# Two shared experts with their inner units on the partitions: a four-layer gated model on one core

## The chip, the cores and the metric

The kernel runs on one core of a Trainium2 chip. The metric is the device time of one execution in microseconds (us), the median of several runs. Engines are named as in the profile: PE (TensorE: matrix products and transposes), PEld (its weight loads), DVE (VectorE), ACT (ScalarE), POOL (GpSimd) and SP (SyncE, which issues DMAs here). All products of the parts below are in fp32, which the profile counts as two PE instructions for each product.

## What is computed

2048 tokens of 512 channels pass four gated layers. Each adds `tanh(g) * attention(layernorm(x))` and then `tanh(g) * ffn(layernorm(x))`. Layer 0 has a quantised cross-attention and LoRA experts, layer 1 a linear attention and 64 experts, layer 2 an attention over channels and a dense network, layer 3 a recurrence and 8 experts. What matters here are the two feed-forward parts with experts. In layer 1 (E = 64 experts, 8 chosen per token, 176 inner units, 256 tokens per expert at most):

```python
def _shared_mlp(x, sh_gate, sh_up, sh_down):          # 512 -> 176 -> 512
    return jax.nn.silu(x @ sh_gate) * (x @ sh_up) @ sh_down
topk_idx, topk_w = _route(x, router_weight, e_bias)
moe_out = _moe_experts(x, topk_idx, topk_w.astype(x.dtype), w_gate, w_up, w_down)
out = moe_out + _shared_mlp(x, sh_gate, sh_up, sh_down)
```

and in layer 3 (8 experts, 2 chosen per token, 352 inner units; the shared expert has 2 x 352 = 704):

```python
y = jnp.einsum('ne,enh->nh', combine, eo)             # routed experts
sh = jax.nn.silu(x @ sw_gate) * (x @ sw_up)           # 512 -> 704
y = y + sh @ sw_down                                  # 704 -> 512
```

## The kernel before

The program is written in three stages, `front()` (layer 0), `middle()` (layer 1) and `back()` (layers 2 and 3). Tokens are worked on in four blocks of 512 (`BLK`), each of four tiles of 128 (`TB`); the residual stream x stays in SBUF. A scheduler places the instructions of each engine from the order in which the program issues them and from their dependencies. The author steers it by generators that are advanced by hand (`step`), by `behind(one, other)`, which fixes the order of two instructions without a wait, and by priorities.

Layer 1 in `middle()`. `attend1(blk, step)` runs the attention of a block and calls `step()` after each piece. `step()` advances `work()`, which for each half block (256 tokens, q = 0 to 6) that has left the attention runs `route1(q)`: layer norm, storing the normed tokens to `xnd` in DRAM, filling the same rows of two result arrays `acc[0]`, `acc[1]` with zeros (32 DMAs of 256 KB in all, on SP's queue), transposing the tokens into `tokens[blk]`, router logits, the choice of eight experts on DVE, and the indirect writes of the choices to `table` in DRAM, issued by POOL (L904). After q = 1 `work()` runs `shared1(0)`, and `attend1(1)` gets a `step` that advances twice for that. When the four blocks are through, `two` (`shared1` of blocks 1 and 2) is interleaved with `route1(7)`, the last half block, whose table writes end the routing. Then the whole table is loaded (`slots`), cast to `who` (L991), and the first tokens are gathered by POOL (`xg<-xnd,who`, L1007). The 64 experts follow, two tiles of 128 slots each (`Tile`, `down1`); their results are added by POOL's accumulating DMAs to `acc` (L1053). A remainder of 48 of the 176 inner units is multiplied there for two tiles side by side, at rows 0 and 64 of the array (L1044). After the experts comes `shared1(3)` with weights loaded again (`again`, on ACT's queue), and `combine()` in `back()` adds the two result arrays to x (L1104).

`shared1` itself, per block: the 176 units are taken as two halves of 88 (`I1H`), which lie on the partitions of the result. Per half four products for the gate and four for the up part (K = 128 each, 88 columns of weights stationary, 512 tokens moving), a silu on ACT, a product on DVE; then per tile of tokens two down products with K = 88 and an addition to x on DVE (L186).

Layer 3 in `back()`. While `ffn2` of layer 2's last block and the shared tiles run on PE, the attention tail of a block, `tail(blk)` (the recurrence `xattn3` on DVE, POOL and ACT, then `route`), is advanced by `step(n)`. `tail(3)` is left when the dense network is through; over it the first `SH0 = 6` shared tiles are issued, with `step(5)` at each `gate_up`, then `step(1000)` ends the tail. Then `cnt` and `pos` (the count of tokens per expert, on PE), the computation of each token's row, 32 table writes on POOL (L1533), the load of `slots`, the cast to `who` (L1552). `SH1 = 3` shared tiles are issued behind it. Then 39 routed tiles (`NS3`): each loads its expert's weights (`w<-in_w,wrow`, 2.2 MB, POOL, a ring of four) and gathers its 128 tokens (L1565), transposes them, runs `tile3`, and adds its result to the output by an accumulating indirect DMA (L1575). After each fifth routed tile one shared tile follows, seven in all.

`tile3` keeps tokens on the partitions: `gate_up` takes a tile of 128 tokens as the stationary operand and moves 352 weight columns, 8 products; a silu on ACT (L1425) and a product with the scale on DVE (L1427) give `h`; `transposed` makes three PE transposes (L1434) and two copies (L1436 on DVE, the other on ACT) of it; `down` makes three products of 512 columns, and `evac` copies the result, by turns on DVE and ACT (L96, L98), before the DMA that adds it to the output (L1465 for shared tiles). The down products of a tile are issued after the next tile's gate and up. A shared tile is two such parts with 352 units each: 16 products, six transposes, six down products.

Pools that count: PSUM has four banks of 512 columns for `mm`, two for transposes (`tr`) and two for `ac` (down products of layer 3); `t2` has eight SBUF buffers of 2 KB per partition, used by all stages for short-lived tiles; `wpool` and `b8` have six of 8 KB each.

Of the kernel before, what the change touches and what calls it, by code (L numbers as in the profile page):

```python
# [31 lines left out]
I1H = I1 // 2  # L32
# [4 lines left out]
SH0, SH1 = 6, 3  # L37
# [6 lines left out]
def flamingo_kernel(ctx: ExitStack, tc: tile.TileContext, a):  # L44
# [533 lines left out]
    def middle():  # L578
        with ExitStack() as st:
# [36 lines left out]
            zero = lp.tile([P, C], F32, tag="zero", name="zero")  # L616
            nc.gpsimd.memset(zero, 0.0)
            empty = lp.tile([P, P, 2], F32, tag="slots", name="empty")
# [8 lines left out]
            shg = rwsh[:, KC * E1 : KC * (E1 + I1)].rearrange("p (k o) -> p k o", k=KC)  # L627
            shu = rwsh[:, KC * (E1 + I1) : KC * (E1 + 2 * I1)].rearrange("p (k o) -> p k o", k=KC)
            for dst, key in ((rw, "rwT1"), (shg, "shg1"), (shu, "shu1")):
                nc.sync.dma_start(dst, a[key].rearrange("p (k o) -> p k o", k=KC))  # L630
            shd = lp.tile([I1H, 2, C], F32, tag="shd1", name="shd1")
# [166 lines left out]
            def route1(q):  # L798
# [4 lines left out]
                if q % 2 == 0:  # L803
                    pool, tag = (wpool, "w") if blk == 1 else (b8, "b8")
                    tokens[blk] = pool.tile([P, KC, BLK], F32, tag=tag, name=f"xnT_f1{blk}")
                xnT = tokens[blk][:, :, ts(q % 2, S)]
                for i in range(2):
                    t = ti + i
                    one = nc.sync.dma_start(xnd[ts(t, P), :], xns[i])
                    for u in range(2):  # L810
                        behind(nc.sync.dma_start(acc[u][ts(t, P), :], zero), one, "not all of them at once")
                    transpose4(xnT[:, :, ts(i, P)], xns[i], f"f1{q}_{i}")
# [104 lines left out]
            def shared1(blk, shg, shu, after=None):  # L917

                xnT = tokens[blk]
                hT = [t2.tile([P, BLK], F32, tag="t2", name=f"shT{blk}_{h}") for h in range(2)]  # L920
                for h in range(2):
                    pg = mmtile(f"shg{blk}_{h}")
                    pu = mmtile(f"shu{blk}_{h}")
                    for ps, wt in ((pg, shg), (pu, shu)):
                        one = matmul_k(
                            ps[:I1H, :], [wt[:, k, ts(h, I1H)] for k in range(KC)], [xnT[:, k, :] for k in range(KC)]
                        )
                        if after is not None:
                            behind(one, after, "beside the sum of the results")
                        yield  # L930
                    act = t2.tile([P, BLK], F32, tag="t2", name=f"sha{blk}_{h}")
                    nc.scalar.activation(act[:I1H, :], pg[:I1H, :], AF.Silu)
                    nc.vector.tensor_tensor(hT[h][:I1H, :], pu[:I1H, :], act[:I1H, :], ALU.mult)
                    yield
                for i in range(TB):
                    ps = mmtile(f"shd{blk}_{i}")
                    matmul_k(ps, [hT[h][:I1H, ts(i, P)] for h in range(2)], [shd[:, h, :] for h in range(2)])
                    t = blk * TB + i
                    last_add[:] = [add_scaled(t, ps, tg[:, 5:6])]
                    yield  # L940

            def work():

                for q in range(2 * NB - 1):
# [3 lines left out]
                    if q == 1:  # L948
                        yield from shared1(0, shg, shu)
# [7 lines left out]
            for blk in range(NB):  # L957
                attend1(blk, (lambda: (step(), step())) if blk == 1 else step)
# [4 lines left out]
            two = (x for blk in range(1, NB - 1) for x in shared1(blk, shg, shu))  # L963
# [12 lines left out]
            again = l2.tile([P, 2, KC, I1], F32, tag="shgu1", name="shgu1")  # L976
            for g, key in enumerate(("shg1", "shu1")):
                nc.scalar.dma_start(again[:, g], a[key].rearrange("p (k o) -> p k o", k=KC))


            slots = lp.tile([P, P, 2], F32, tag="slots", name="slots")
# [8 lines left out]
            who = lp.tile([P, P], I32, tag="who", name="who")  # L990
            one = nc.vector.tensor_copy(who, slots[:, :, 0])  # L991
            behind(one, last_add[0], "the table comes late")

            I1R = I1 - P
            rows_of = (slice(0, I1R), slice(HD * 2, HD * 2 + I1R))

# [95 lines left out]
            for _ in shared1(NB - 1, again[:, 0], again[:, 1], latest[0]):  # L1092
# [168 lines left out]
    def back():  # L1261
        with ExitStack() as st:
# [140 lines left out]
            for h in range(2):  # L1403
                for kk in range(2):
                    w = late.tile([P, 4 * I3], F32, tag=f"shgu{h}_{kk}", name=f"shgu{h}_{kk}")
                    nc.sync.dma_start(w, a["shgu3"][h][:, kk * 4 * I3 : (kk + 1) * 4 * I3])
                    shgu += [w[:, k * 2 * I3 : (k + 1) * 2 * I3].rearrange("p (g i) -> p g i", g=2) for k in range(2)]
# [7 lines left out]
            def gate_up(xTt, wgu, scale, name):  # L1415
# [11 lines left out]
                one = nc.vector.scalar_tensor_tensor(h, act, scale, pu[:, 0:I3], ALU.mult, ALU.mult)  # L1427
                return h, one

            def transposed(h, name):  # L1430
# [4 lines left out]
                hT = late.tile([P, 3, P], F32, tag="hT3", name=f"hT3_{name}", bufs=4)  # L1435
# [4 lines left out]
            def down(name, hTs, wds, add):  # L1440
                ps = ac.tile([P, C], F32, tag="ac", name=f"d3_{name}")
                pairs = [(hT[:cn, n, :], wd[n][:cn]) for hT, wd in zip(hTs, wds) for n, (_, cn) in enumerate(chunks)]
                matmul_k(ps, [l for l, _ in pairs], [r for _, r in pairs])
# [7 lines left out]
            def tile3(name, parts, wds, add):  # L1451
                hs = []
# [238 lines left out]
```

## Time and profile before

The median of three runs is 2926.47 us (2926.19 to 2926.68). The profile is of another execution, of 2930.48 us.

| | us |
|---|---|
| median of the runs | 2926.47 |
| profiled execution, its own time | 2930.48 |
| its span on the page | 2928.6 |
| mean granted clock of TensorE | 0.967 |
| PE busy | 2713.0 (93%) |
| layer 1's experts, 1043.9 to 1621.2 | 577.3 |
| layer 3's routed tiles, 2472 to 2922 | 450.0 |

The span begins at 0 with the first instruction that the profiler saw. A row of a timeline gives the start, the time that the group took, engine, line, operation, output and inputs, partitions and columns, the count, and in brackets the idle time of the engine before it and what ended that. In a table of windows each row is a stretch of the span, with its length and the busy time of each engine in it. The tenths of section 2 of the page cut the span into 40 slices of 73.2 us. The busy time of PE is modelled, so distances between starts are the better measure of what a product takes.

### The profile page before, as it was taken

What the parts mean: (1) busy time and instruction counts of PE and PEld (TensorE: products, weight loads), DVE (VectorE), ACT (ScalarE), POOL (GpSimd) and SP (SyncE); (2) the same over time, 40 slices, a digit from 0 to 9 for tenths busy, and PEclk for the clock granted to TensorE, in tenths of its full rate; (3) what the DMA queues carried; (4) which work ended last, traced back from release to release, by engine and by line L of the source; (5) the groups of instructions that cost most, each with busy time, mean ns of one, the idle gap of its engine ahead of it and who ended that gap; (6) DMA issues with size and microseconds to landing.
All of it is one profiled execution on the core that took longest, in us unless ns stands there. A gap on an engine that the chain in (4) does not pass through costs nothing. (4 is left out here: it accounts for less than half of the span.)

```text
span 2928.6 us, 30661 instructions
## 1 busy us (share of the span) xinstructions
PE 2713.0 (93%) x10918; PEld 1478.7 (50%) x10918; DVE 1315.5 (45%) x3574; ACT 711.0 (24%) x1616; POOL 942.4 (32%) x849
## 2 busy tenths in 40 slices
PE   7888978899899989999999899898999888999998
PEld 3444544464555445555555344344444554555554
DVE  7566665353556522222222631767566861111111
ACT  2534343011111123333333211222222220111111
POOL 1102010104324455555555110322223326333232
PEclk9999989899899999999999999999999999999999
DMA  5000000110101168999998722121221214777775
GB/s 198 22 4 19 28 25 19 45 54 6 58 23 37 54 189 204 216 227 224 215 221 204 226 87 75 40 101 36 83 90 36 94 44 159 241 258 235 225 249 142
DMA packets 104746, 345.09 MB, mean 118 GB/s; under 512 B 22426, under 2 KB 24858, under 8 KB 96787
## 3 DMA queue, kind: packets, MB, share of 16 engines
q0 software_dynamic: 50448, 168.71, 23.3%
q1 hardware_dynamic: 51123, 169.19, 16.8%
q10 hardware_dynamic: 3024, 5.24, 0.5%
q8 instruction: 87, 1.43, 0.2%
q14 instruction: 64, 0.52, 0.1%
HBM read 283.42 MB, written 69.80 MB: 121 GB/s over the span
## 5 line engine op out<-in xcount | busy, mean ns | idle before, releaser
L175 PE MATMUL gu<-w,eb 128*128 128x352 f32 x1024 | 326.5, 462 | 0.0
L1053 POOL DMA_INDIRECT acc<-eb,who x128 | 203.9, 1593 | 197.7 <-DVE eb L96 174.5
L175 PE MATMUL h2p<-xnT_f,p 128*128 128x512 f32 x512 | 227.4, 600 | 6.0 <-issue 3.9
L175 PEld LDWEIGHTS gu<-w,eb 128*128 128x128 f32 x1024 | 185.7, 191 | 83.6 <-issue 2.3
L175 PE MATMUL o2f<-p,h 128*128 128x512 f32 x512 | 226.1, 597 | 0.7 <-ACT h L1166 0.7
L471 ACT ACTIVATE pr<-pr,n 128x256 f32<-128x256 f32 x256 | 127.9, 501 | 157.2 <-DVE n L466 151.8
L175 PEld LDWEIGHTS h2p<-xnT_f,p 128*128 128x128 f32 x512 | 97.5, 192 | 125.1 <-issue 120.7
L175 PEld LDWEIGHTS o2f<-p,h 128*128 128x128 f32 x512 | 97.1, 191 | 120.3 <-issue 116.8
L904 POOL DMA_INDIRECT table<-pay,rowi x128 | 125.7, 982 | 93.2 <-DVE hit L895 47.8
L1007 POOL DMA_INDIRECT xg<-xnd,who x128 | 135.1, 1055 | 58.2 <-PE ehp L1033 27.3
L1427 DVE SCALAR_TENSOR_TENSOR h_r<-a_r,slots,u_r 128x352 f32<-128x352 f32 x39 | 22.6, 580 | 225.2 <-ACT a_r L1425 118.3
L159 PEld LDWEIGHTS tr_xg<-ident,xg 128*128 128x128 f32 x668 | 78.2, 142 | 87.3 <-issue 78.9
L186 DVE SCALAR_TENSOR_TENSOR x<-o2f,tg,x 128x512 f32<-128x512 f32 x64 | 47.8, 748 | 165.2 <-PE o2f L175 165.2
L175 PE MATMUL d_r<-w,hT_r 128*128 128x512 f32 (+1 forms) x234 | 115.3, 606 | 7.3 <-DVE hT_r L1436 6.0
L1044 PE MATMUL ed<-w,eb 128*128 128x512 f32 x256 | 120.8, 593 | 0.9 <-DVE eb L1034 0.9
L159 PE MATMUL tr_xg<-ident,xg 128*128 128x128 f32 x668 | 104.9, 280 | 17.4 <-DMA xg<-xnd,who 17.4
L1421 PE MATMUL g_r<-w,xgT 128*128 128x352 f32 x312 | 119.0, 463 | 0.0
L1421 PE MATMUL u_r<-w,xgT 128*128 128x352 f32 x312 | 118.0, 460 | 0.0
L96 DVE COPY eb<-ed 128x512 f32<-128x512 f32 x64 | 44.3, 692 | 158.5 <-PE ed L1044 158.5
L1166 ACT ACTIVATE h<-h2p,b 128x512 f32<-128x512 f32 x64 | 43.1, 687 | 290.1 <-PE h2p L175 289.9
L1023 DVE SCALAR_TENSOR_TENSOR eb<-eb,slots,gu 128x176 f32<-128x176 f32 x128 | 50.2, 392 | 139.1 <-ACT eb L1022 139.1
L478 PE MATMUL pt<-ident,pr 128*128 128x128 f32 x512 | 88.1, 293 | 19.9 <-ACT pr L471 16.2
(396 smaller groups left out, 4984.7 us busy)
## 6 DMA issues: line engine op xcount, KB each, us to landing
w<-in_w SPq DMA_DIRECT2D x64, 960.0 KB, 6.9
p<-in_p SPq DMA_DIRECT2D x64, 512.0 KB, 5.5
xnd<-xn_f SPq DMA_DIRECT2D x32, 256.0 KB, 2.7
acc<-zero SPq DMA_DIRECT2D x32, 256.0 KB, 3.0
more<-acc SPq DMA_DIRECT2D x32, 256.0 KB, 4.8
wd<-in_wd SPq DMA_DIRECT2D x64, 96.0 KB, 6.1
x<-in_x SPq DMA_DIRECT2D x16, 256.0 KB, 7.0
ctxTb<-in_ctxT SPq DMA_DIRECT2D x4, 1024.0 KB, 5.0
```

What stands on the lines that cost most here:

```text
L96: nc.vector.tensor_copy(dst, src)
L159: nc.tensor.transpose(ps[:, k, :], src[:, ts(k, P)], ident)
L175: one = nc.tensor.matmul(ps, lhsT[k], rhs[k], start=(k == 0), stop=(k == n - 1))
L186: return nc.vector.scalar_tensor_tensor(xt[i], ps, scale, xt[i], ALU.mult, ALU.add)
L471: nc.scalar.activation(pr[:, nt, :], pr[:, nt, :], AF.Exp, bias=n16[:, nt, h : h + 1], scale=-1.0, accum_out=s16[:, nt, h : h + 1],)
L478: nc.tensor.transpose(pt_ps[:, lt, nt, :], pr[:, nt, ts(lt, P)], ident)
L904: one = nc.gpsimd.indirect_dma_start(out=table[:, :], out_offset=bass.IndirectOffsetOnAxis(ap=row_i[:, i, j : j + 1], axis=0), in_=pay[:, ...
L1007: nc.gpsimd.indirect_dma_start(out=xg, out_offset=None, in_=xnd[:, :], in_offset=bass.IndirectOffsetOnAxis(ap=who[:, c : c + 1], axis=0), ...
L1023: nc.vector.scalar_tensor_tensor(self.h, self.h, slots[:, c, 1:2], gu[:, I1 : 2 * I1], ALU.mult, ALU.mult)
L1044: one = nc.tensor.matmul(ps[n], t.hT[rows, k, :], wd[k][rows], start=(k == 0), stop=(k == 1))
L1053: nc.gpsimd.indirect_dma_start(out=acc[n][:, :], out_offset=bass.IndirectOffsetOnAxis(ap=who[:, t.c : t.c + 1], axis=0), in_=t.x, in_offse ...
L1421: nc.tensor.matmul(ps[:, 0:I3], xTt[:, k, :], wgu[k][:, g, :], start=(k == 0), stop=(k == KC - 1))
```

## The change

Both shared experts are put in one form: inner units on the partitions, 128 at a time, 512 tokens moving, and the units that are left over from gate and up joined in one product.

- Layer 1, `shared1`: 128 units of gate, 128 of up, and one product of 112 columns that holds the last 48 of gate (rows 0 to 47 of the result), 16 columns of zeros, and the last 48 of up (rows 64 to 111). Down goes by pairs of tiles: one full product of K = 128 for each, and the two of K = 48 side by side at rows 0 and 64 (`behind` fixes their order). The host lays out the weights as `shgu1` (one load for gate and up) and `shd1` with the last 48 rows twice.
- Block 0's `shared1` is taken out of `work()` and put ahead of blocks 1 and 2 in `two`, behind the attention; `attend1(1)` has a single `step`. `tokens[0]` has a buffer of its own, `tokens[1]` one of `wpool`, the others of `b8`.
- Layer 3, `shared3`: a generator of eight pieces per block. The first is the joined remainder (64 of gate, 64 of up: four products of 512 columns, `step(2)`), five are 128 units of gate and up (eight products, `step(5)` each), two are the down products of a pair of tiles (ten full, two of K = 64 side by side, `step(3)`). No transposes. `SH0 = 14` pieces stand over `tail(3)`, `SH1 = 8` after the table, then one after each third routed tile, which is ten. `tile3` serves routed tiles alone.
- The zero tile of layer 1 is a short-lived one of `t2`, and the zero fills of `acc` copy from the 128 zero rows at the end of `xnd`, DRAM to DRAM. `slots` and `who` are in the pool `l2`, which opens after the attention.

```diff
-SH0, SH1 = 6, 3
+SH0, SH1 = 14, 8
...
-            zero = lp.tile([P, C], F32, tag="zero", name="zero")
+            zero = t2.tile([P, C], F32, tag="t2", name="zero")
...
-                    pool, tag = (wpool, "w") if blk == 1 else (b8, "b8")
+                    pool, tag = ((lp, "tokens"), (wpool, "w"), (b8, "b8"), (b8, "b8"))[blk]
...
-                        behind(nc.sync.dma_start(acc[u][ts(t, P), :], zero), one, "not all of them at once")
+                        fill = nc.sync.dma_start(acc[u][ts(t, P), :], xnd[NT : NT + P, :])
+                        behind(fill, one, "not all of them at once")
...
+                pg = products("shg", slice(0, P))
+                nc.scalar.activation(act[0], pg, AF.Silu)
+                yield
+                pu = products("shu", slice(P, 2 * P))
+                nc.vector.tensor_tensor(hT[0], pu, act[0], ALU.mult)
+                yield
+                ps = products("shr", slice(2 * P, I1W))
+                nc.scalar.activation(act[1][rest1, :], ps[0:I1R, :], AF.Silu)
+                for n in range(2):
+                    pick = lambda x: x.rearrange("p (t n q) -> p t n q", n=2, q=P)[:, :, n]
+                    nc.vector.tensor_tensor(
+                        pick(hT[1][rows_of[n], :]), pick(act[1][rest1, :]), pick(ps[rest1, :]), ALU.mult
+                    )
+                yield
+                for i in range(0, TB, 2):
+                    ps = [mmtile(f"shd{blk}_{i + n}") for n in range(2)]
+                    last = None
+                    for k in range(2):
+                        for n in range(2):
+                            rows = rows_of[n] if k else slice(0, P)
+                            one = nc.tensor.matmul(
+                                ps[n], hT[k][rows, ts(i + n, P)], shd[rows, k, :], start=(k == 0), stop=(k == 1)
+                            )
+                            if last is not None:
+                                behind(one, last, "remainders side by side")
+                            last = one
+                    latest[:] = [last]
+                    for n in range(2):
+                        last_add[:] = [add_scaled(blk * TB + i + n, ps[n], tg[:, 5:6])]
                     yield
...
                     yield from route1(q)
-                    if q == 1:
-                        yield from shared1(0, shg, shu)
...
-                attend1(blk, (lambda: (step(), step())) if blk == 1 else step)
+                attend1(blk, step)
...
-            two = (x for blk in range(1, NB - 1) for x in shared1(blk, shg, shu))
+            two = (x for blk in range(NB - 1) for x in shared1(blk, shgu))
...
-            for _ in shared1(NB - 1, again[:, 0], again[:, 1], latest[0]):
+            for _ in shared1(NB - 1, again, latest[0]):
...
+            def shared3():
+                half = [slice(FD * n, FD * n + FD) for n in range(2)]
+                scale = tg[:, 7:8]
+                for blk in range(NB):
+                    xb = [xT[blk][:, k, :] for k in range(KC)]
+                    hT = late.tile([P, 6, BLK], F32, tag="shT3", name=f"shT3_{blk}")
+                    for m in (5, *range(5)):
+                        nm = f"{blk}_{m}"
+                        act = t2.tile([P, BLK], F32, tag="t2", name=f"sa3_{nm}")
+                        pg = mmtile(f"sg3_{nm}")
+                        if m == 5:
+                            matmul_k(pg, [w[:, 10 * P :] for w in shgu], xb)
+                            nc.scalar.activation(act[half[1], :], pg[half[0], :], AF.Silu)
+                            for n in range(2):
...
+                            step(2, one)
+                        else:
+                            pu = mmtile(f"su3_{nm}")
+                            for ps, c in ((pg, m), (pu, m + 5)):
+                                matmul_k(ps, [w[:, ts(c, P)] for w in shgu], xb)
+                            nc.scalar.activation(act, pg, AF.Silu)
+                            one = nc.vector.scalar_tensor_tensor(hT[:, m, :], act, scale, pu, ALU.mult, ALU.mult)
+                            step(5, one)
+                        if later:
+                            down(*later.pop())
+                        yield
+                    for i in range(0, TB, 2):
+                        ps = [ac.tile([P, C], F32, tag="ac", name=f"sd3_{blk}_{i + n}") for n in range(2)]
+                        last = None
+                        for m in range(6):
+                            for n in range(2):
+                                rows = half[n] if m == 5 else slice(0, P)
+                                one = nc.tensor.matmul(
+                                    ps[n], hT[rows, m, ts(i + n, P)], shd[m][rows, :], start=(m == 0), stop=(m == 5)
+                                )
+                                if last is not None:
+                                    behind(one, last, "remainders side by side")
+                                last = one
+                        for n, copy in enumerate((nc.vector.tensor_copy, nc.scalar.copy)):
+                            t = blk * TB + i + n
+                            y = t2.tile([P, C], F32, tag="t2", name=f"ys3_{t}")
+                            one = copy(y, ps[n])
+                            if n == 0:
+                                step(3, one)
+                            nc.gpsimd.dma_start(out=a["out"][ts(t, P), :], in_=y, accum_op=ALU.add)
+                        yield
...
-            for t in range(SH0):
-                shared(t)
+            more = shared3()
+            for n in range(SH0):
+                next(more)
             step(1000)
...
             for n in range(SH1):
-                shared(done)
-                done += 1
+                next(more)
             for n in range(NS3):
                 routed(n)
-                if n % 5 == 4 and done < TT:
-                    shared(done)
-                    done += 1
-            while done < TT:
-                shared(done)
-                done += 1
+                if n % 3 == 2:
+                    next(more, 0)
+            for _ in more:
+                pass
             down(*later.pop())
```

## Prediction

> **What bounds the kernel now.** I read the page first, then a table of windows by stage, then the timelines of the places where TensorE stands still. The chain that ended last is cut off after its last DMA here, so the bound is read stage by stage.
>
> ```profile
> PE 2713.0 (93%) x10918; PEld 1478.7 (50%) x10918; DVE 1315.5 (45%) x3574; ACT 711.0 (24%) x1616; POOL 942.4 (32%) x849
> ...
> PE   7888978899899989999999899898999888999998
> ```
>
> TensorE is the bound, with dips in the tenths. The windows give span, then busy us of PE, PEld, DVE, ACT, POOL, then granted clock, DMA share, GB/s: attention blocks 1, 2, 3 of layer 1 (blocks of 512 tokens), the wait for its expert table, its experts, then layer 3's attention tail, its table, its routed tiles.
>
> ```profile
> 650.19:781.01 130.82, 120.01 (x581) 68.10 (x580) 65.71 (x291) 17.56 (x28) 46.36 (x49) 0.90 0.10 33
> 781.01:881.71 100.70, 91.73 (x534) 54.71 (x532) 53.32 (x222) 13.70 (x24) 32.51 (x34) 0.97 0.09 32
> 881.71:985.05 103.34, 92.92 (x533) 56.21 (x532) 60.37 (x254) 15.09 (x25) 39.56 (x44) 0.95 0.15 49
> 985.05:1043.91 58.86, 46.67 (x131) 20.04 (x129) 27.88 (x138) 5.80 (x8) 36.48 (x38) 0.92 0.26 84
> 1043.91:1621.20 577.29, 576.43 (x2298) 331.89 (x2297) 157.55 (x382) 187.90 (x447) 331.25 (x250) 1.00 0.89 211
> ...
> 2282.76:2411.09 128.33, 112.15 (x420) 69.00 (x419) 90.00 (x151) 34.35 (x49) 42.44 (x39) 0.93 0.20 56
> 2411.09:2472.00 60.91, 47.11 (x151) 27.14 (x151) 11.24 (x39) 6.81 (x15) 42.25 (x43) 0.91 0.37 112
> 2472.00:2922.00 450.00, 438.80 (x1487) 255.51 (x1486) 80.16 (x149) 62.21 (x149) 136.67 (x116) 1.00 0.72 231
> ```
>
> Block 1, which holds shared block 0, takes 29 us more than its neighbours. The experts and the routed tiles are TensorE-bound; the two table stages are not. PE's timeline (start, duration, group, idle before it) at the table wait of layer 1, and POOL's:
>
> ```profile
> 1023.11 7.29 PE L175 MATMUL shd<-shd,shT 88*128 88x512 f32 x16
> 1042.04 1.94 PE L159 MATMUL tr_xg<-ident,xg 128*128 128x128 f32 x8 [11.64 <-DMA xg<-xnd,who]
> ```
>
> ```profile
> 1029.82 0.97 POOL L904 DMA_INDIRECT table<-pay,rowi  x1 [0.30 <-issue]
> 1034.63 1.06 POOL L1007 DMA_INDIRECT xg<-xnd,who  x1 [3.83 <-DVE who L991]
> ```
>
> The shared products end 11.64 us before the first gathered tokens: POOL's 32 table writes, 1.27 us apart from 990.2 on, set the end of this stage. In layer 3 likewise (PE's timeline):
>
> ```profile
> 2448.36 5.32 PE L175 MATMUL d_s<-shd,hT_s 128*128 128x512 f32 x12
> 2461.72 1.54 PE L1434 MATMUL h3t_s<-ident,h_s 128*128 128x128 f32 x6 [8.04 <-DVE h_s L1427]
> ...
> 2470.89 1.09 PE L159 MATMUL tr_xg<-ident,xg 128*128 128x128 f32 x4 [5.76 <-DMA xg<-xnd,who]
> ```
>
> Of all filler, only what TensorE does outside these two waits is worth its time. Last, the price of two 48-row products side by side (PE's timeline):
>
> ```profile
> 1619.11 1.10 PE L1044 MATMUL ed<-w,eb 128*128 128x512 f32 x2 [0.47 <-DVE eb L1034]
> 1620.14 1.13 PE L1044 MATMUL ed<-wd,eb 48*128 48x512 f32 x4
> 1621.20 3.67 PE L175 MATMUL shg<-xnT_f,shgu 128*88 128x512 f32 x8
> 1624.70 1.88 PE L175 MATMUL shu<-xnT_f,shgu 128*88 128x512 f32 x4
> ```
>
> From start to start: a 512-column fp32 product (two instructions) takes 0.86-0.88 us whether 88 or 128 rows or columns are used; the pair of 48-row products takes 1.06 for both.
>
> **What the Trainium skill says.** "TensorE: Matmul & The Clock Gate", Part 3: products on different row groups run at once, the pack lasting about as long as one. The trace agrees in part: 1.06 us against 1.72 for two, but 0.86 for one; I use 1.06. Part 1 of that page: after an idle window of about 3.4 us the clock falls to half. The trace has clocks of 0.90 to 0.92 in just the windows with long idles. Its architectural detail: ACT's and DVE's queues are strict FIFO. It agrees: h_s stands 8.04 us behind the cast of `who`. "DMA: Bandwidth & Descriptors", rules for kernel authors: an accumulating DMA must wait for the earlier one's semaphore; POOL shows that wait at 2561.50 and 2570.64 (2.38 and 2.83 us, released by out_dram).
>
> **Part by part**, on the profiled execution's 2930.5 us (span 2928.6 and 1.9 around it), which lies 4.0 above the median.
>
> *1. Products of layer 1's shared expert.* Per block 24 products of 0.86 = 20.6 us (16 gate and up, 8 down) become 12 + 4 of 0.86 and 2 pairs of 1.06: 15.9. So 4.75 us per block, 19.0 over four.
>
> *2. Block 0's shared work leaves attention block 1.* Its 20.6 us of PE go, and the doubled step with them, which put DVE work of routing and sharing into the attention's own chain and let the clock fall. If block 1 becomes like 2 and 3 (mean 102.0) it saves 130.8 - 102.0 = 28.8. Bounds 20.6 (PE work only) and 31; I take 28.8.
>
> *3. Table wait of layer 1.* Filler goes from two blocks (41.2) to three short ones (3 x 15.85 = 47.5): 6.3 us more, inside the 11.64 idle. Cost 0; without that cover 6.3. Block 0's two products for h, silus and four adds (0.75 each) now stand on DVE and ACT among route 7's; behind them waits the last `hit` and behind that POOL's writes. The writes need 41 us, and the hits come a microsecond or two ahead of POOL by my order of DVE: 0, bounds -3 and +5.
>
> *4. Zero fills* go from SBUF to DRAM, 32 of 256 KB on SP (now 3.0 us to landing). DRAM to DRAM is not in the trace. They are read first after 1054 us, and the last is issued before 985, so 0 to 10 us each would be hidden; a ctxT load (1 MB, 5.0 us) stands behind some. SP waited 307 us for xn_f in this stage, so the queue has room. I take 0; bounds 0 and +5. The single load of `again` on ACT's queue for two, and four loads of layer 3's shared weights for four, cost the same.
>
> *5. Block 3's shared work after the experts.* 4.75 us less before the adds of the results, which stand behind its adds on DVE; TensorE resumes at 1650.44 after 8.15 us for xn_a. If the results' loads (4.8 us) come late instead, the gain is lost: 0 to 4.75; I take 4.
>
> *6. Products of layer 3's shared expert.* Before, per tile of 128 tokens: 16 of 352 columns at 0.592 = 9.47, six transposes of 0.11, six down of 0.86 = 5.15: 15.3; 244.5 for 16. After, per block: 44 of 0.86 and two times (10 full of 0.86 and one pair of 1.06) = 57.1; 228.2 for four. So -16.3: gate and up cost the same, transposes and remainders go. On DVE two copies (0.42) and two products (0.58) per tile become 5 wide products and 2 half ones per block: less.
>
> *7. Under the attention tail* 14 steps (94.8 us) stand for six tiles (91.7). The chain over DVE, POOL and ACT (about 20.8 us for each chunk of channels) sets this stage, and steps come at each product as before. The copy of a tile's result holds DVE until its products end, 4.3 us before; it now waits for a pair of 9.64 but seldomer. I take -2; bounds -8 and +8.
>
> *8. Table wait of layer 3.* From `cnt` to `who` is 50 us of POOL in both. Eight steps (57.0 us) replace three tiles (45.8). Some 11 us of idle move ahead of `who`, since the wide products' DVE steps stand behind its cast, and four PSUM banks fill; then about 10 us of ready products cover the gather, whose 5.76 us of idle go. Take -1; bounds -3 and +5.
>
> *9. Routed tiles.* Shared work here falls from 7 x 15.3 = 107.0 to 228.2 - 94.8 - 57.0 = 76.4: -30.6, all in a stage with PE at 438.8 of 450. Fewer waits of d_s for hT_s (2.4 us in this stage): -1. But the last nine tiles have no shared step between them. One then takes 8.69 us on PE, and its accumulate waits for the one before: issues at 2550.75, 2561.50, 2570.64, 2578.67 are 9.3 apart where weights are loading. Five such tiles x 0.6 = +3; bounds 0 and +10.
>
> Sum: -28.8 + 0 + 0 - 4 - 2 - 1 - 28.6 = -64.4. The profiled 2930.5 becomes 2866; at the median 2862.
>
> **The rivals.**
> *Only products count.* The 19.0 + 16.3 = 35.3 us of TensorE work go, and no idle is filled: block 1's surplus moves to block 2 or to the table wait, where route 7's hits come late. For it: DVE is a strict queue with new work there. Against: 11.64 us of idle await filler. 2926.5 - 35.3 = 2891.
> *New waits in layer 3.* The tail +8 and the end +10 in place of -2 and +3: 17 less, 2879. For it: DVE 90 of 128 us in the tail, and copies queued behind longer products. Against: fewer DVE instructions.
> *Slower: the accumulate chain.* Each of 39 tiles waits for its forerunner's landing, from about 9.3 us now. With layer 1 giving 32.8, the kernel is slower by over 0.2% once routed tiles take 450 + 32.8 + 5.9 = 489 us, 12.5 us each; at 13 us it ends near 2926.5 - 32.8 + 57 = 2951. For it: DMA share rises from 0.72 to 0.72 x 450/421 = 0.77. Against: 8 to 10.8 us is all I see, and at the end, with the weights loaded, the tiles follow at 8.7.
> *It doesn't do what it says.* If the order keeps block 0 in the attention and the shared tiles' idles, 2926. The build's order of instructions speaks against it: the shared transposes are gone and PE's instructions fall.
>
> **How the numbers follow.** Forecast 0.60, only products 0.15, new waits 0.16, slower 0.05, nothing 0.04. A measurement here tells about 0.2% (5.9 us) from no change. Faster 0.91, same 0.04, slower 0.05. The range runs from 2846 (block 1 at -31, combine -4.75, tail -6, table -3, routed -36, rounded) to 2892, just past the products alone.
>
> **What would show it.** Block 1's window at 100 to 104 us with no shg in it (step 2). Idle of 4 to 7 us ahead of the first tr_xg in layer 1, at the same distance from block 3's end (3). Shared blocks of 15.9 (1, 5). `cnt` within 8 us of its place after the combine (7); idle near 11 us before `who` and none for xg (8); routed window 418 to 424 (9). Wrong if route 7's last table write slips by over 5 us, if PE waits at each shared pair, or if out_dram releases every accumulate.

## The result and the profile after

The changed kernel takes 2891.94 us (median of four runs, 2890.79 to 2895.47) against 2926.33 for the kernel before: a ratio of 0.9885, 95% interval 0.9868 to 0.9902. It is faster by some 34 us, about half of the 64 that the sum had given, at the very edge of the range, which ended at 2892. The profiled execution has a span of 2893.7 us, 34.9 less than before.

The page after, the rows that answer to those shown of before:

```profile
PE 2676.9 (93%) x10630; PEld 1427.0 (49%) x10630; DVE 1312.1 (45%) x3542; ACT 698.7 (24%) x1574; POOL 940.9 (33%) x849
...
PE   7889978899898999999999899898999988999998
```

TensorE has 36.1 us less to do and the span is 34.9 shorter, as if only the products had counted. The stages tell otherwise. Windows after (span, then busy us of PE, PEld, DVE, ACT, POOL, granted clock, DMA share, GB/s): attention blocks 1 to 3, the table wait of layer 1, then the attention tail of layer 3, its table up to the cast of `who`, from there to the first routed gate, and the routed tiles:

```profile
650.53:753.91 103.38, 92.52 (x533) 56.16 (x532) 60.38 (x256) 13.70 (x24) 39.71 (x41) 0.95 0.13 42
753.91:857.36 103.45, 92.99 (x533) 57.08 (x532) 60.46 (x256) 13.80 (x24) 39.53 (x41) 0.95 0.10 32
857.36:962.10 104.74, 94.27 (x533) 57.59 (x532) 60.19 (x254) 15.08 (x25) 39.56 (x44) 0.93 0.15 49
962.10:1021.98 59.88, 53.59 (x148) 22.20 (x146) 32.46 (x149) 6.99 (x10) 34.80 (x36) 0.97 0.23 71
2253.14:2396.33 143.19, 128.54 (x372) 63.58 (x371) 94.80 (x152) 33.93 (x37) 42.23 (x39) 0.92 0.20 63
2396.33:2446.14 49.81, 39.85 (x98) 16.78 (x96) 7.99 (x30) 5.43 (x8) 36.17 (x38) 0.96 0.20 54
2446.14:2461.89 15.75, 13.74 (x28) 6.08 (x29) 3.59 (x6) 0.60 (x1) 7.33 (x8) 0.80 1.03 360
2461.89:2887.00 425.11, 403.74 (x1311) 223.28 (x1311) 69.96 (x127) 54.03 (x127) 135.81 (x116) 1.00 0.75 240
```

Cut at the same instructions in both traces (wo is the attention's output product, tr_xg the transposes of the first gathered tokens, gu and ed the experts' gate/up and down products, o2f the last products of layer 2's dense network, d_r a routed tile's down products):

| stage | before | after | difference | forecast |
|---|---|---|---|---|
| attention block 1 | 130.8 | 103.4 | -27.4 | -28.8 |
| attention blocks 2 and 3 | 204.0 | 208.2 | +4.2 | 0 |
| last wo product to first tr_xg | 57.4 | 59.9 | +2.5 | 0 |
| experts of layer 1 (gu to the last ed) | 576.8 | 575.2 | -1.5 | 0 |
| to the first product of layer 2 | 29.8 | 25.6 | -4.1 | -4 |
| layer 2 | 626.2 | 628.0 | +1.8 | 0 |
| last o2f product to cnt | 134.4 | 143.2 | +8.7 | -2 |
| cnt to the first routed gate | 62.4 | 65.6 | +3.2 | -1 |
| routed tiles, first gate to last d_r | 446.4 | 422.4 | -24.0 | -28.6 |

Of the parts that moved by design, layer 1 gives 26 us where 33 were counted, and layer 3 gives 12 where 31.6 were. Layer 2 is no part of the change; over the profiles of all kernels here it takes either about 626 or 628.0 us.

Where it falls short can be read in four places, three in layer 3 and one in layer 1. First, DVE in the third chunk of the recurrence (start, duration, group, idle before and what ended it):

```profile
2317.35 3.34 DVE L1265 RECIPROCAL den<-den 128x512 f32<-128x512 f32 x1
...
2327.59 0.69 DVE L1245 TENSOR_TENSOR_SCAN aa<-ex,ev 128x256 f32<-128x256 f32 x1 [4.66 <-POOL ev L1242]
2337.84 0.69 DVE L1524 COPY ys<-sd 128x512 f32<-128x512 f32 x1 [9.56 <-PE sd L1515]
2338.45 0.68 DVE L1245 TENSOR_TENSOR_SCAN aa<-ex,ev 128x256 f32<-128x256 f32 x1
...
2346.55 3.35 DVE L1265 RECIPROCAL den<-den 128x512 f32<-128x512 f32 x1 [0.38 <-POOL bb L1221]
```

Between the two halves of one scan stands the copy of a shared result, and it waits 9.56 us for a pair of down products. PE shows why that pair ends so late: it stood 4.20 us for the copy of the pair before it, and ten instructions of the next piece came between its first two instructions and the rest.

```profile
2321.92 1.17 PE L1515 MATMUL sd<-shd,shT 128*128 128x512 f32 x2 [4.20 <-DVE ys L1524]
2322.88 6.15 PE L176 MATMUL sg<-xnT_f,shgu 128*128 128x512 f32 x10
2328.87 8.95 PE L1515 MATMUL sd<-shd,shT 128*128 128x512 f32 x22
```

From this reciprocal to the next it takes 29.2 us. DVE of the kernel before, with 21.5 us between the same two and its longest wait for a shared result later, in the routing:

```profile
2332.91 3.35 DVE L1245 RECIPROCAL den<-den 128x512 f32<-128x512 f32 x1 [1.16 <-POOL bb L1201]
...
2354.43 3.35 DVE L1245 RECIPROCAL den<-den 128x512 f32<-128x512 f32 x1 [0.67 <-POOL bb L1201]
...
2408.24 0.69 DVE L96 COPY y_s<-d_s 128x512 f32<-128x512 f32 x1 [4.30 <-PE d_s L175]
```

Second, PE ahead of the first routed tile:

```profile
2435.51 1.45 PE L176 MATMUL sg<-xnT_f,shgu 128*128 128x512 f32 x3
2447.03 6.43 PE L176 MATMUL su<-xnT_f,shgu 128*128 128x512 f32 x8 [10.08 <-DVE shT L1504]
...
2461.89 0.83 PE L1440 MATMUL g_r<-w,xgT 128*128 128x352 f32 x2 [1.12 <-issue]
```

The idle of 10.08 us was forecast; that the next eight instructions then take 6.43 us instead of 3.60, at a granted clock of 0.80 in this window (0.50 from 2442.33 to 2452.57), was not.

Third, PE in the routed stage around a shared piece:

```profile
2563.93 0.86 PE L1440 MATMUL g_r<-w,xgT 128*128 128x352 f32 x2 [0.78 <-DVE xgT L97]
...
2569.66 0.55 PE L1453 MATMUL h3t_r<-ident,h_r 128*128 128x128 f32 x3 [0.73 <-DVE h_r L1446]
```

Two waits that the kernel before doesn't have: over the routed stage g_r waits 4.7 us for xgT and h3t_r 5.1 us for h_r, and in the kernel before both are 0. Fourth, in layer 1, DVE at the end of the table wait:

```profile
1016.73 1.41 DVE L187 SCALAR_TENSOR_TENSOR x<-shd,tg,x 128x512 f32<-128x512 f32 x2 [1.56 <-PE shd L957]
1018.05 0.22 DVE L1014 CAST who<-slots 128x128 int32<-128x128 f32 x1
```

and of the kernel before:

```profile
1030.43 0.75 DVE L186 SCALAR_TENSOR_TENSOR x<-shd,tg,x 128x512 f32<-128x512 f32 x1 [0.97 <-PE shd L175]
1034.13 0.23 DVE L991 CAST who<-slots 128x128 int32<-128x128 f32 x1 [2.94 <-DMA slots<-table]
```

After the change no idle stands before the cast: the table was there, and the cast waited its turn behind the additions of shared block 2.

### The profile page after: what moved, and what is told of

Its sections match the earlier page's. It is cut to its first block, busy times and chain, and to the rows that moved or that the text cites. A ratio compares the mean times of both kernels' runs of the same rounds, so it can differ in the third digit from the quotient of the medians.

```text
span 2893.7 us, 30023 instructions
## 1 busy us (share of the span) xinstructions
PE 2676.9 (93%) x10630; PEld 1427.0 (49%) x10630; DVE 1312.1 (45%) x3542; ACT 698.7 (24%) x1574; POOL 940.9 (33%) x849
## 3 DMA queue, kind: packets, MB, share of 16 engines
q1 hardware_dynamic: 47440, 169.38, 16.9%
## 5 line engine op out<-in xcount | busy, mean ns | idle before, releaser
L1027 POOL DMA_INDIRECT xg<-xnd,who x128 | 134.3, 1049 | 58.9 <-PE ehp L1053 27.4
```

Source lines behind the costliest of these rows:

```text
L1027: nc.gpsimd.indirect_dma_start(out=xg, out_offset=None, in_=xnd[:, :], in_offset=bass.IndirectOffsetOnAxis(ap=who[:, c : c + 1], axis=0), ...
```

## The experiments

The theory after the result: the products cost what was counted, and the rest was lost to queues, because an instruction that the table, the recurrence or a routed tile needs stands behind an instruction that waits for a shared product. The rival: TensorE's work alone decides, so idle that is taken away in one place comes back in the next. Every kernel below is the changed kernel with the edit shown. Ratios are to the kernel before on the same chip. The control of the changed kernel (

> The changed kernel itself, as the control on the same chip as the three below: 0.9885 of the kernel before if the chip is like that of the first result.

) gave 2891.07 us and 0.9878 (0.9861 to 0.9894), on the chip on which e4, e5, e10, e11 and e12 ran too. e1, e2, e3 and e6 ran on another chip, where the kernel before takes 2929.36 us and no control ran; they are compared with one another and with the first result.

**Layer 1's cast ahead of the last additions (e1).**

```diff
-            behind(one, last_add[0], "the table comes late")
+            behind(one, last_mult[0], "the table comes late")
+            cast[:] = [one]
+            for _ in two:
+                pass
...
                         last_add[:] = [add_scaled(blk * TB + i + n, ps[n], tg[:, 5:6])]
+                        if cast and after is None:
+                            behind(last_add[0], cast[0], "behind the cast")
```

> The changed kernel, with the cast of layer 1's table (who) ordered ahead of the last four additions of shared block 2 on DVE, where it stood behind them. If the held cast made the table wait longer (59.9 us from the last wo product to the first tr_xg), it falls by the 5.4 us that the cast stood in the queue, to about 54.5. If the gathers are then held up by the weight loads that SP issues at the same moment, as in the kernel before (7.9 us from cast to transposes against 3.9 in the changed one), only 1.4 us are won, about 58.5. Whole time: 1 to 5 us less than the changed kernel.

2890.43 us, 0.9869 (0.9849 to 0.9889): in the whole time no difference that the times can show. The stage does: `who` comes 50.6 us after the last wo product (55.9 in the changed kernel), and the first transposes after 58.3 (59.9). So the cast was held for 5.3 us, and only 1.6 of them are won. POOL and PE of this kernel tell where the rest went: the first gather is issued at 1012.58 and lands for

```profile
1019.78 1.79 PE L160 MATMUL tr_xg<-ident,xg 128*128 128x128 f32 x8 [3.72 <-DMA xg<-xnd,who]
```

7.2 us later, beside the weights that SP issues at about that time; in the changed kernel it takes 3.4 us from issue to transpose (1018.54 to 1021.98), where SP had issued the weights 6 us before the gather. That the weights slow the gather is argued from this coincidence; no run changed their order.

**Down products kept for the next routed tile (e3).**

```diff
                             step(5, one)
-                        if later:
-                            down(*later.pop())
                         yield
```

> The changed kernel, but a shared piece of gate and up no longer issues the down products of the routed tile before it; they stay for the next routed tile, where they stand between its gate/up and its transposes. If the two waits after such a piece (0.78 us for xgT and 0.73 for h_r, six times each) come from the missing cover, both go: 9 to 10 us less in the routed stage and in the whole time. If the stage is bound by the loads of weights or by the accumulating DMAs, the waits move there and the time changes by less than 3.

2880.71 us, 0.9835 (0.9815 to 0.9854): 11 us below the first result of the changed kernel, and 9.7 to 12.7 below e1, e2 and e6 on the same chip. The routed stage goes from 422.4 to 412.7. PE of this kernel at the same place:

```profile
2557.55 0.60 PE L160 MATMUL tr_xg<-ident,xg 128*128 128x128 f32 x4
2557.98 1.02 PE L176 MATMUL d_r<-w,hT_r 128*128 128x512 f32 x2
2559.00 0.86 PE L1440 MATMUL g_r<-w,xgT 128*128 128x352 f32 x2
```

A down product stands between transposes and gate and covers the copy of xgT; both waits are gone. The shared piece had spent the down products where nothing had to be covered.

**Copies of the shared results on ACT (e2).** A first attempt on the tail:

```diff
-                        for n, copy in enumerate((nc.vector.tensor_copy, nc.scalar.copy)):
+                        if blk == 0:
+                            step(3)
+                        for n, copy in enumerate((nc.scalar.copy if blk == 0 else nc.vector.tensor_copy, nc.scalar.copy)):
...
+                    one = nc.gpsimd.dma_start(out=a["out"][ts(t, P), :], in_=y, accum_op=ALU.add)
+                    behind(one, chunk[0], "not ahead of the recurrence")
```

> The changed kernel, with the copies of shared block 0's results on ACT alone, and the output DMAs of its second pair put on POOL behind the recurrence's chunk. If the tail was made longer by DVE and POOL standing behind a pair of down products (9.56 us in the third chunk), the distance of the second to the third reciprocal falls from 29.2 us to about 20, and the count (cnt) comes 8 to 10 us earlier; the whole time falls by 6 to 9. If the tail is bound by TensorE, which has some 13 us more shared work in it than before, cnt moves by less than 2 us.

2893.45 us, 0.9882 (0.9862 to 0.9902): nothing, and 32.2 us from the second to the third reciprocal where about 20 were expected. The hold had only changed its queue. DVE of this kernel:

```profile
2323.88 1.24 DVE L1245 TENSOR_TENSOR_SCAN aa<-ex,ev 128x256 f32<-128x256 f32 x2
2338.00 0.99 DVE L1496 SCALAR_TENSOR_TENSOR shT<-sa,tg,sg 64x256 f32<-64x256 f32 x2 [12.88 <-ACT sa L1493]
```

DVE now waits for a silu, which stands on ACT behind the copies, which wait 12.06 us for the second pair of down products, which itself started 7.96 us late because its banks were not copied out. Taken alone, this run speaks for the rival.

**Fewer shared pieces over the tail (e6).** `SH0, SH1 = 12, 10` in place of 14 and 8.

> The changed kernel with 12 pieces over the attention tail and 10 behind the table in place of 14 and 8: 13.7 us of TensorE work less in the tail, both pairs of down products still in it. If TensorE bounds the tail, cnt comes 8 us earlier or more. If DVE behind the down products does, cnt moves by 0 to 3 us. Behind the table there are 13.7 us more of products than before, which the idle of 10 us cannot take, since it comes from the cast and not from missing work: whole time between 5 less and 8 more.

2891.06 us, 0.9875 (0.9854 to 0.9897), and 139.98 us from the last o2f product to cnt, against the control's 139.97. The run tells nothing on the rival: the scheduler put the same 194 gate and up and 48 down instructions ahead of cnt, filling in from the pieces behind it, so the work over the tail was not changed. It serves as a repeat: DVE again waits 9.34 us for the second pair. (The changed kernel's first profile has 143.2; 2.4 of the 3.2 us between them lie ahead of the first reciprocal.)

**The pairs without a wait between them, and late copies (e9).**

```diff
+                        if blk == 0 and i:
+                            ps = [mmtile(f"sd3_{blk}_{i + n}") for n in range(2)]
...
+                        if owed and m in (5, 2):
+                            sent(0, *owed.pop(0))
```

`sent` makes the copies and issues the output DMAs, behind the recurrence's chunk on POOL.

> The changed kernel, with the second pair of down products of shared block 0 in two banks of the mm pool, so that it does not wait for the first pair's copies, and with the copies and output DMAs of both pairs put two to four pieces later, behind the recurrence's chunk on DVE and POOL. If the third chunk is long because DVE, ACT and POOL queue behind these pairs, the distance of the second to the third reciprocal falls from 29.2 us to 19 to 22 and cnt comes 7 to 10 us earlier; whole time 6 to 10 less. If TensorE's greater work bounds the tail, less than 2.

This run and a second one fell on chips on which the kernel before takes 2977 to 2978 us. Ratio 0.9792 (0.9776 to 0.9808) and again 0.9791; from the last o2f product to cnt 131.7 and 130.1 us, with 21.5 from the second to the third reciprocal, both times. On a chip like that of the first result, within e10 below, the stage takes 129.97 against the control's 139.97. DVE of that kernel at the place shown above:

```profile
2320.81 1.24 DVE L1251 TENSOR_TENSOR_SCAN aa<-ex,ev 128x256 f32<-128x256 f32 x2
2325.53 0.99 DVE L1502 SCALAR_TENSOR_TENSOR shT<-sa,tg,sg 64x256 f32<-64x256 f32 x2 [3.48 <-ACT sa L1499]
```

The wait is 3.48 us where it was 9.56 and 12.88. The tail of e10 holds the same 372 matrix instructions as that of the changed kernel and is 10.0 us shorter than the control's, so TensorE's work did not bound it; the queues behind the down products did. The edit has three parts (banks of their own, later copies, later output DMAs), and no run tells which of them is needed.

**Block 0's shared work back under the attention (e5).**

```diff
                     yield from route1(q)
+                    if q == 1:
+                        yield from shared1(0, shgu)
...
-                attend1(blk, step)
+                attend1(blk, (lambda: (step(), step())) if blk == 1 else step)
...
-            two = (x for blk in range(NB - 1) for x in shared1(blk, shgu))
+            two = (x for blk in range(1, NB - 1) for x in shared1(blk, shgu))
```

> Block 0's shared work of layer 1 back under attention block 1, against the control of the same chip. If it costs there what it did before: 18 to 19 us more. If only work counts: within 3 us of the control.

2909.28 us, 0.9945 (0.9928 to 0.9961): 18.2 above the control. Its four runs lie far apart, between 2903.46 and 2913.44, and the profiled one, at 2903.46, is only 12.4 above that of the control, so the size is less sure than the sign. Windows of blocks 1 to 3:

```profile
648.50:773.10 124.60, 113.67 (x574) 66.11 (x573) 65.93 (x297) 17.44 (x28) 46.24 (x48) 0.90 0.11 35
773.10:873.80 100.70, 91.65 (x534) 54.72 (x533) 52.89 (x219) 13.69 (x24) 32.71 (x35) 0.97 0.10 32
873.80:977.10 103.30, 92.83 (x534) 56.16 (x533) 60.38 (x254) 15.08 (x25) 39.57 (x44) 0.95 0.15 49
```

Block 1 takes 20.9 us more than the control's 103.8 for 15.9 us of products, its clock is 0.90 again, and the next two take 100.7 and 103.3, just what the kernel before shows. So block 2's 2.8 us belong to the move: in the kernel before, and here, it has 0.79 us of idle ahead of tr_a (the transposes of the attention's input), where the changed kernel has 3.5 to 3.7 in each of these blocks. Over the three blocks together this kernel takes 328.6 us and the control 312.1, so most of block 1's surplus over the products is given back by its neighbours: 16.5 us for 15.9. What the move gains is that the products then cost little in the table wait, which here is only 1.6 us shorter than the control's. The doubled step, the clock and the work on DVE are not told apart. (Two runs on the chips with 2977 us gave 0.9949 and 0.9921.) It also shows that the zero fills from DRAM, which this kernel has too, cost the attention blocks nothing. No run has the fills from SBUF.

**Layer 3's cast behind the shared steps (e4).**

```diff
-SH0, SH1 = 14, 8
+SH0, SH1 = 14, 9
...
             for n in range(SH1):
                 next(more)
+                if n == 7:
+                    one = nc.vector.tensor_copy(who, slots[:, :, 0])
+                    behind(one, last_h[0], "the table comes late")
```

The cast in its old place, ahead of the routed tiles, is taken out.

> Layer 3's cast (who) behind the DVE steps of eight shared pieces, SH1 = 9, against the control of the same chip. If TensorE's idle ahead of the cast comes only from the steps behind it: 12 to 14 us less than the control. If the shared steps are late for another reason (a buffer or an engine that the table writes hold), the cast is late with them, the idle moves, and the time is within 3 us of the control.

2892.09 us, 0.9883 (0.9866 to 0.9899): nothing, though one piece more is done before the routed tiles. (Two earlier runs, on the chips with 2977 us, gave 0.9826 and 0.9831 and had stalls on ACT and DVE in this very stage; no control ran there.) PE and POOL of this kernel:

```profile
2441.69 9.81 PE L1516 MATMUL sd<-shd,shT 128*128 128x512 f32 x24
2462.61 1.12 PE L160 MATMUL tr_xg<-ident,xg 128*128 128x128 f32 x4 [11.12 <-DMA xg<-xnd,who]
```

```profile
2440.40 1.05 POOL L1618 DMA_INDIRECT w<-in_w,wrow  x1 [0.30 <-issue]
2441.75 0.98 POOL L1618 DMA_INDIRECT w<-in_w,wrow  x1 [0.30 <-issue]
2443.04 0.94 POOL L1618 DMA_INDIRECT w<-in_w,wrow  x1 [0.30 <-issue]
2444.28 0.95 POOL L1627 DMA_INDIRECT xg<-xnd,who  x1 [0.30 <-issue]
```

The idle ahead of the cast is gone and stands behind the shared work instead, 11.12 us: three loads of expert weights, 2.2 MB each, were issued ahead of the first gather, and its tokens came 18 us after its issue. (Three loads are 6.6 MB; at the 391 to 429 GB/s that this stretch moved, they alone take 15 to 17 us, an estimate.) The theory was right on the idle and blind for the next queue.

**The same with the gather first (e12).**

```diff
+                if gathered:
+                    behind(load, gathered[0], "the first tokens ahead of the weights")
```

> As e4: layer 3's cast behind the DVE steps of eight shared pieces, SH1 = 9; and in addition the weight loads of all routed tiles but the first ordered on POOL behind the first gather, where e4 had three of them ahead of it. If the queue on POOL made the first tokens late: they land within 10 us of the cast, under the pair of down products; 61 to 63 us from cnt to the first routed gate against 73.7 in e4 and 65.4 in the control, and 12 to 14 us less than the control, whose ratio to the kernel before was 0.988: about 0.983. If the second tile's weights are late in their place, TensorE waits there and the ratio stays at 0.987 or above.

2878.24 us, 0.9828 (0.9811 to 0.9844), 2927.61 for the kernel before. From cnt to the first routed gate 62.0 us with nine pieces done, against 73.7 in e4 and 65.4 with eight in the control: 12.8 us below the control in all. POOL and PE of this kernel; PE goes without idle from the pair to the transposes:

```profile
2446.81 1.06 POOL L1631 DMA_INDIRECT xg<-xnd,who  x1 [3.36 <-issue]
2448.17 0.99 POOL L1620 DMA_INDIRECT w<-in_w,wrow  x1 [0.30 <-issue]
```

```profile
2444.91 9.81 PE L1516 MATMUL sd<-shd,shT 128*128 128x512 f32 x24
2454.65 0.66 PE L160 MATMUL tr_xg<-ident,xg 128*128 128x128 f32 x4
```

**Together.** e10 is e1, e3 and e9; e11 is e10 with e12.

> Three of the edits at once: layer 1's cast ahead of the last additions, the down products kept for the next routed tile, the down pairs of shared block 0 with late copies. If the waits are independent: 1.5 + 11 + 11 = 23.5 us less than the control. If what is won in one is waited for in the next: less than 15.

2868.88 us, 0.9805 (0.9789 to 0.9822): 22.2 below the control, where the parts, as the earlier runs had them (1.5, 11 and 11), add up to 23.5.

> The edits of e10 (ratio 0.9805) and of e12 together. If they are independent: 13 us less than e10, a ratio near 0.976. If the weight loads that are moved back make the routed tiles wait: no less than e10.

2855.75 us, 0.9756 (0.9740 to 0.9772): 13.1 below e10 and faster than both kernels. An earlier sum without the order on POOL (

> The changed kernel with four edits at once: the cast of layer 1 ahead of the last additions, down products kept for the next routed tile, layer 3's cast behind the shared steps with SH1 = 9, and the down pairs of shared block 0 with late copies. If the four waits are independent: 1.5 + 11 + 13 + 8 = 33.5 us less than the changed kernel, about 2858. If the time won in one place is waited for in the next, about 2875.

) gave 0.9744 (0.9728 to 0.9760) and again 0.9754 on the chips with 2977 us, where e9 alone had 0.9792. With the same shared products the changed kernel has lost 35.3 us in all, nearly the sum of the parts: these waits are independent, and the rival falls.

## Why the prediction was off

**Products (steps 1 and 6): right.** Shared block 3 of layer 1 takes 16.3 us from 1600.01 to the end of its last product, where it took 21.1 (15.9 and 20.6 were counted). In layer 3 the routed stage has 34.1 us less of shared products by count (110.5 to 76.4), where 30.6 was counted. Packing two 48-row products cost what the trace of before had shown.

**Block 1 (step 2): right** in size, -27.4 for -28.8, and putting it back costs that block 20.9 us for 15.9 of work (e5). What was missed is that its neighbours profited from it: blocks 2 and 3 take 4.2 us more now, so that their mean of 102.0 was too low a mark. Over the three blocks the move gives 23.2 us for 20.6 of products. So most of the 8.2 us that step 2 put down to the doubled step, DVE and the clock was not there to be had; which of the three made the rest stays open. The reading that low clocks stand "in just the windows with long idles" was too neat as well: block 2 of the kernel before has an idle of 5.51 us and a clock of 0.97, block 1 none above 3.75 and 0.90.

**Table wait of layer 1 (step 3): wrong, small.** "6.3 us more, inside the 11.64 idle. Cost 0" took TensorE's idle for the cover. But the cast is ordered behind the last addition of the shared work, and DVE's own idle ahead of it was 2.94 us in the kernel before. That was the cover. The additions held the cast for 5.3 us (e1), and POOL's last table write came 1.1 us later than before; +2.5 came through, since the gathers took 3.9 us from the cast to the transposes where they took 7.9 before.

**Zero fills and the adds after the experts (steps 4 and 5): right,** 0 and -4.1.

**The attention tail (step 7): the failed step with the largest share.** The mechanism was named, "it now waits for a pair of 9.64 but seldomer", and sized at -2, with +8 as its bound; it came to +8.7 in the profiled execution and +5.5 in the control. Of the rival "new waits in layer 3" this half came true, and its other half, +10 at the end, did not. The mis-sized term is the hold: 9.56 us where 4.3 were before, and its place. The copy of the kernel before stood in routing, near the end; this one splits the recurrence, whose queues on DVE, ACT and POOL then all wait; TensorE too waits there for the copy of the first pair (4.20 us). Undoing it gives 10.0 us (control to e10). By count 102.7 us of shared products stand ahead of cnt, not 94.8 (the kernel before has 89.6), since the scheduler draws some of the next pieces forward. The second chunk also takes 22.0 us instead of 16.9; e9 leaves that as it is, and its cause was not tested.

**Table of layer 3 (step 8): right on the idle, wrong on its price.** 11 us of idle ahead of `who` were forecast, 10.08 came, and the gather was covered as said. ("h_s stands 8.04 us behind the cast" misread its line: 8.04 us is TensorE's wait for h_s, which DVE ran right behind the cast, 2461.08 after 2460.97.) But the first products after the idle lost 2.8 us (6.43 us for 3.60, granted clock 0.80): the Trainium skill has it in "TensorE: Matmul & The Clock Gate", Part 1, that the clock falls to half after an idle window, and this trace agrees: it is 0.50 from 5.4 us after the idle's start until 5.5 us after its end. e4 shows the same behind its 11.12 us of idle. The sum took these products at full speed. (The kernel before has two such stretches here too, 2458.10 to 2464.92 and 2468.34 to 2475.16; in e12, without the idle, there is none.) In sum the stage took 3.2 us more, where 1 less was forecast.

**Routed tiles (step 9): two errors.** The added 3 us for the accumulate chain did not come: the last seven distances from one tile's transposes to the next tile's are 8.69 or 8.70 us. And "fewer waits: -1" was the wrong sign: TensorE's idle in this stage rose from 9.7 to 20.3 us, because a shared piece spends the down products that cover the next tile's copies: 9.8 us of it are the two waits shown. e3 makes the stage 9.7 us shorter.

So of the 29.5 us missing, 10.7 lie in step 7, 5.6 in step 2 with the blocks behind it, 4.6 in step 9, 4.2 in step 8 and 2.5 in step 3; the rest, about 2, is what layer 2 (+1.8) and other stages differ by from one execution to the next. "Only products count" named 2891 and was hit by accident: block 1 gave more than its products, and other places gave less.

## What to carry to other kernels

When work is moved into an idle, ask what else is queued behind its last instruction: the cover is the idle of the engine that carries the next step's release, here 2.94 us on DVE, and not TensorE's 11.64. A larger product makes a longer hold for everything that stands behind its copy, so here the wide pieces wanted their copies late and banks of their own. And a filler must leave the pipeline's own cover alone: products that hide a copy are worth more where they hide it than anywhere else.

## What the runs showed of the hardware

- A gather of 128 rows that POOL issued behind three loads of 2.2 MB came 18 us after its issue (e4); issued ahead of them, it came within 7.9 us, under the pair of products (e12). Whether it stood behind them in the queue or only shared the engines' rate with them, these runs do not tell.
- The result and three sets of runs have 2926 to 2929 us for the kernel before; two other sets have 2977 to 2978, with waits of some 20 us on ACT and DVE beside POOL's table writes that the profile puts down to no engine of the core. Their cause stays open, and no profile of the kernel before was taken there.
- TensorE's granted clock was 0.50 around idles of 10.08 us (after) and 11.12 us (e4), up to 5.5 and 8.0 us beyond their end, and the products in it took nearly twice their time: 6.43 us for eight instructions where 3.60 is usual.
